# Cross-attention and a mixture of experts on one core: exponentials half a batch behind the maxima, and a first and a due step for every other stage

## The chip, the cores and the metric

One core of a Trainium2 chip (trn2). The engines named below are PE (TensorE, matrix products and transposes), DVE (VectorE), ACT (ScalarE), POOL (GpSimd) and SP (SyncE, which here only issues DMAs). The metric is the time of one execution on the device in microseconds (us), as the median over runs. All data is 32-bit float.

## The reference, cut to what matters

`x` is 8 batches of 256 tokens of width 512, `ctx` the same. Norms have no learned scale.

```python
x = x + xattn(layernorm(x), ctx, ctx)   # q: 32 heads of 16; k, v: 8 groups, each shared by 4 heads
                                        # softmax(q k^T / 4) v, then @ Wfc.T + bfc
h = layernorm(x)
scores = softmax(h @ gate_weight.T)     # 8 experts in 4 pairs: the two best pairs, the two best experts
routed = sum over the two experts of  w * (silu(h @ g.T) * (h @ u.T)) @ d.T     # inner width 352
shared = (silu(h @ sg.T) * (h @ su.T)) @ sd.T                                   # inner width 704
x = x + routed + shared
```

## The kernel before, in words

Order of execution on PE, ACT, DVE and SP is the order in which the program issues instructions (`manual_schedule`); each engine works its own queue in that order. All work of the first stage is done batch by batch (256 tokens, two row tiles of 128), and the kernel interleaves several batches by hand.

**The stages of one batch.**
- `project(b)`: normalizes x (moments, a power on POOL, two rows), products for keys and values (`pkv`), transposes (`tx`, `tk`), products for queries (`pq`, 512 wide), transposes (`tq`) into `qT`. Keys and queries carry a 17th row: in `kT` it is all ones, in `qT` it is filled later with minus the row maximum, so that the exponential needs no separate subtraction.
- `maxima(b)`: eight units per batch. A unit makes 1024 scores per query row group (L598, into the one PSUM buffer `ps_s` of four banks), and DVE reduces them to negated row maxima `nm` (L606). After every second unit `place` transposes these (`tn`) and DVE adds them into `qT` (L588).
- `softmax(b)`: eight units. A unit makes transposed scores (L667, into the same `ps_s`), ACT takes the exponential (L675, 128x2048), PE multiplies with the values (`av`, L626, `values`); every second unit DVE copies the sum (`avs`), PE transposes it (`to`), and DVE divides by the row sum (`divide`). Here `av` of unit k is issued after the scores of unit k+1.
- `close(b)`: loads x again as `acc`, POOL adds the bias, transposes of the attention output (`too`), the output product (`fc`, L701), DVE adds it to `acc`, then `layernorm`, transposes (`th`) into `hT`.
- `router(b)`: gate product (`lg`, 16 products of 8 columns), some twenty small DVE operations for the choice of experts, a product for the places (`pos`), more small DVE operations, then four indirect DMAs from POOL that scatter the rows to the experts' lists in DRAM (`rows`).
- `feed.pieces(b)`: the shared feed-forward: six pairs of products (`gu`, 3.45 us of PE each), ACT's tanh, two DVE operations, then two output products (`o`, L166), a DVE add and the write of `y`.

PSUM for everything but scores and `av` comes from `ps_m`, three buffers in turn.

**What sets the order.** The main loop runs b = 0 to 7, each with eight steps. A step issues one unit of `maxima(b + 1)` and one of `softmax(b)`, so exponentials follow the maxima by a whole batch; before b = 0 stands a loop of `maxima(0)` with `project(1)` alone. The other stages are generators that yield pieces of 0.44 to 1.72 us of PE time. A `Filler` holds those of this b (`feed.pieces(b - 2)`, `router(b - 2)`, `project(b + 2)`, `close(b - 1)`), spreads their whole cost evenly over the eight steps (0.6 of a step's share after the maxima's scores, 0.4 at the step's end), takes the stage that is least advanced, and drains what is left after the eighth step. `copy.free` says whether PSUM copies go to ACT (first part of a step) or DVE (second part). A piece that yields True leaves a product open, and the same stage goes on.

**The end.** After b = 7 come `close(7)`, `router(6)`, `router(7)` and `feed.pieces(6)`, `plan()` (some 35 DVE operations that make the tables of the routed stage, and eight more scatters), and `routed`: 39 tiles of 128 rows, each an expert's rows fetched with a DMA (`xs`, whose row number is read from a table), transposed (`rx`), multiplied (`rg`, `ro`) and added into `y` by an indirect DMA. `feed.pieces(7)` is threaded through its first lines (L331 and on).

Of the kernel before, what the change touches and what calls it, by code (L numbers as in the profile page):

```python
# [37 lines left out]
P = 128  # L38
# [22 lines left out]
PAUSE = 0.01, False  # L61

# [118 lines left out]
class Filler:  # L181
# [3 lines left out]

    def __init__(self, *stages):
        self.stages = [[g, total, 0.0, ahead] for g, total, ahead in stages]
        self.credit = 0.0
        self.last, self.open = None, False

    def total(self):
        return sum(s[1] for s in self.stages)

    def step(self):
        s = self.last
        if not self.open:
            others = [t for t in self.stages if t is not self.last]
            s = min(others or self.stages, key=lambda t: t[2] / (t[1] * t[3]))
        piece = next(s[0], None)
        if piece is None:  # L200
            self.stages.remove(s)
            return
        cost, self.open = piece
        s[2] += cost
        self.credit -= cost
        self.last = s

    def fill(self, amount):
        self.credit += amount
        while self.stages and self.credit > 0:  # L210
            self.step()

    def drain(self):
        self.fill(1e9)
# [13 lines left out]
def routed(ctx, tc, ps_m, wgu, wd, ident, rows, t_exp, t_row, t_one, out, tail, right):  # L228
# [104 lines left out]
    advance(tail, 3)  # L333
# [6 lines left out]
    advance(tail, 12)  # L340
    turn(0)
    for _ in tail:
        pass
# [18 lines left out]


def advance(stage, n):
    for _ in range(n):
        next(stage)


def attention(
# [109 lines left out]
    def layernorm(tiles, b, key, width, bufs):  # L479

        mv = small.tile([P, QC, 2], F32, tag=f"mv{key}", name=f"mv{key}{b}")
        for q in range(QC):
            st = small.tile([P, 6], F32, tag="st", name=f"st{key}{b}_{q}")
            nc.vector.bn_stats(st, tiles[q])
            nc.vector.bn_aggr(mv[:, q], st)
        rstd = small.tile([P, QC], F32, tag=f"rstd{key}", name=f"rstd{key}{b}")
        nc.vector.tensor_scalar(rstd, mv[:, :, 1], EPS, None, ALU.add)
        nc.gpsimd.tensor_tensor(rstd, rstd, mhalf, ALU.pow)
        normed = []
        for q in range(QC):  # L490
            n = small.tile([P, width], F32, tag=f"row{key}", bufs=bufs, name=f"ln{key}{b}_{q}")
            nc.vector.tensor_scalar(
                n[:, :D], tiles[q], mv[:, q, 0:1], rstd[:, q : q + 1], ALU.subtract, ALU.mult
            )
            normed.append(n)
        return normed
# [11 lines left out]
    def project(b):  # L508

        xt, cT = loaded.pop(b)  # L510
        normed = layernorm(xt, b, "a", D, 2)
# [52 lines left out]
        qT = p3.tile([P, NG, GH, S], F32, tag="qT", name=f"qT{b}")  # L564
# [11 lines left out]
    def maxima(b):  # L576


        qT, kT = qTs[b], kTs[b]

        def place(G, j0):
            ps = ps_m.tile([P, 2, S], F32, tag="m", name=f"tn{b}_{G}_{j0}")
            for j in range(2):
                for qc in range(QC):
                    nc.tensor.transpose(
                        ps[:, j, qc * P : (qc + 1) * P], nm[qc][:, G, j0 + j], ident
                    )
            nc.vector.tensor_add(qT[:, G, j0 : j0 + 2], ps, qT[:, G, j0 : j0 + 2])  # L588

        ready = []  # L590
        for G in range(NG):
            for j0 in range(0, GH, 2):
                for qc in range(QC):
                    ps = ps_s.tile([P, 4, 2, S], F32, tag="s", name=f"s1_{b}_{G}_{qc}_{j0}")
                    for j in range(2):
                        for r in range(4):
                            band = slice(32 * r, 32 * r + KA)
                            nc.tensor.matmul(  # L598
                                ps[:, r, j],
                                lhsT=qT[band, G, j0 + j, qc * P : (qc + 1) * P],  # L600
                                rhs=kT[band, G],
                                start=True,
                                stop=True,
                            )
                    to = nm[qc][:, G, j0 : j0 + 2].rearrange("p j (r x) -> p r j x", x=32)
                    nc.vector.tensor_reduce(to[:, :, :, 0], ps, AX.X, ALU.max, negate=True)  # L606
                    yield
                    if ready:
                        place(*ready.pop())
                    yield  # L610
                ready.append((G, j0))
        place(*ready.pop())

    def softmax(b):

        qT, kT, v = qTs.pop(b), kTs.pop(b), vs[b % 3]
        o = [p2.tile([P, D], F32, tag=f"o{qc}", name=f"o{b}_{qc}") for qc in range(QC)]
        os_[b] = o
        avs_ = {}

        def values(G, j0, kc, ex):
            if kc == 0:
                avs_[G, j0] = ps_av.tile([P, 2, S], F32, tag="av", name=f"av{b}_{G}_{j0}")
            av = avs_[G, j0]
            for r in range(4):
                nc.tensor.matmul(  # L626
                    av[32 * r : 32 * r + 32],
                    lhsT=v[:, kc, 4 * G + r],
                    rhs=ex[:, r],
                    start=(kc == 0),  # L630
                    stop=(kc == QC - 1),
                )
            if kc == QC - 1:
                sb = p2.tile([P, 2, S], F32, tag="avs", name=f"avs{b}_{G}_{j0}")
                nc.vector.tensor_copy(sb, av)
                return G, j0, sb

        def divide(G, j0, sb):
            ps = ps_m.tile([P, QC, 2, 4, 32], F32, tag="m", name=f"to{b}_{G}_{j0}")
            for qc in range(QC):  # L640
                for j in range(2):
                    nc.tensor.transpose(
                        ps[:, qc, j].rearrange("p r d -> p (r d)"),
                        sb[:, j, qc * P : (qc + 1) * P],
                        ident,
                    )
            rec = small.tile([P, QC, 2, 4, 1], F32, tag="rec", name=f"rec{b}_{G}_{j0}")
            nc.vector.reciprocal(rec, ps[:, :, :, :, HD : HD + 1])
            half = D // NG
            for qc in range(QC):  # L650
                to = o[qc][:, G * half : (G + 1) * half].rearrange(
                    "p (r j d) -> p j r d", r=4, j=GH
                )
                nc.vector.tensor_mul(
                    to[:, j0 : j0 + 2],
                    ps[:, qc, :, :, :HD],
                    rec[:, qc].to_broadcast([P, 2, 4, HD]),
                )

        behind, done = [], []  # L660
        for G in range(NG):
            for j0 in range(0, GH, 2):
                for kc in range(QC):
                    ps = ps_s.tile([P, 4, 2, S], F32, tag="s", name=f"s2_{b}_{G}_{kc}_{j0}")
                    for r in range(4):
                        band = slice(32 * r, 32 * r + KA)
                        nc.tensor.matmul(  # L667
                            ps[:, r],
                            lhsT=kT[band, G, kc * P : (kc + 1) * P],
                            rhs=qT[band, G, j0 : j0 + 2],  # L670
                            start=True,
                            stop=True,
                        )
                    ex = p2.tile([P, 4, 2, S], F32, tag="ex", name=f"ex{b}_{G}_{kc}_{j0}")
                    nc.scalar.activation(ex, ps, AF.Exp, scale=HD**-0.5)  # L675
                    yield
                    if done:
                        divide(*done.pop())
                    if behind:
                        done.append(values(*behind.pop()))  # L680
                        if done[-1] is None:
                            done.pop()
                    behind.append((G, j0, kc, ex))
                    yield
        last = values(*behind.pop())
        yield
        divide(*last)

    def close(b):
# [4 lines left out]
        o = os_.pop(b)  # L694
        for qc in range(QC):
            oT = p2.tile([P, NC, P], F32, tag="oT", bufs=1, name=f"oT{b}_{qc}")
            transposed(o[qc], oT, f"too{b}_{qc}")
            yield 0.44, False
            ps = ps_m.tile([P, D], F32, tag="m", name=f"fc{b}_{qc}")
# [180 lines left out]
    for _ in project(0):  # L880
        pass
# [3 lines left out]
    for k, _ in enumerate(maxima(0)):  # L885
        if k % 2 == 0:
            other.fill(share)
# [100 lines left out]
```

## Time and profile before

| | us |
|---|---|
| median of 3 runs (1120.47 to 1550.64) | 1124.05 |
| the profiled execution, whole | 1115.04 |
| its span, first to last instruction | 1113.3 |
| PE busy | 1046.5 (94%) |
| DVE busy | 476.9 (43%) |
| ACT busy | 225.3 (20%) |
| POOL busy | 143.4 (13%) |
| mean granted TensorE clock | 0.97 |

The page gives busy times over the whole span and, in 40 slices of 27.8 us, each engine's busy tenths and the clock that PE was granted. Groups of instructions carry the line in the kernel, the engine, what is written from what, and the mean duration; an idle time before an instruction is put down to what released it last. `x8` after a product in the timeline counts 32-bit products twice, as two passes each. PE's records overlap by about 0.1 us, so that the distance from start to start is the price of an instruction in a row of them. Memory traffic is 67 GB/s on average and 14.2% of the DMA engines' time for the main queue.

### The profile page before, as it was taken

To read this page: it belongs to the slowest core of one execution; us is meant where nothing else is said; L and a number is where in the kernel's file an instruction comes from. 1 tells how busy PE (TensorE), PEld (TensorE's weight loads), DVE (VectorE), ACT (ScalarE), POOL (GpSimd) and SP (SyncE) were. 2 spreads that over 40 slices of the span, in tenths; PEclk is the share of its full clock that TensorE was granted. 3 is DMA by queue.
4 is the path that set the end of the run, shared out by engine and by line. 5 is a ranking of instruction groups with operands and counts; after the bars stand their busy time and mean duration, and the time that the engine had idled before them with its cause. 6 is when DMAs were issued, how large, how long until landed. Compare 5 with 4: busy or idle time off the path is not lost. (4 is left out here: it accounts for less than half of the span.)

```text
span 1113.3 us, 13379 instructions
## 1 busy us (share of the span) xinstructions
PE 1046.5 (94%) x5291; PEld 604.2 (54%) x5291; DVE 476.9 (43%) x1082; ACT 225.3 (20%) x276; POOL 143.4 (13%) x168
## 2 busy tenths in 40 slices
PE   6877899999999999999999999999999999999994
PEld 4542435554564555465455464667556566666652
DVE  3743546644654644555455534362122222222221
ACT  2132223222222122122222232110111111111110
POOL 3000000110000011101001101032012121211212
PEclk9988899998999999999899999999999999999998
DMA  5510010110200011101000101128963333233323
GB/s 199 199 38 1 15 44 1 57 40 9 67 4 36 20 58 39 39 1 40 10 29 30 49 1 49 29 82 322 376 201 69 67 60 75 58 77 58 75 32 38
DMA packets 26733, 74.94 MB, mean 67 GB/s; under 512 B 3376, under 2 KB 3376, under 8 KB 25392
## 3 DMA queue, kind: packets, MB, share of 16 engines
q1 hardware_dynamic: 17856, 53.04, 14.2%
q0 software_dynamic: 8816, 21.04, 8.5%
q8 instruction: 43, 0.70, 0.3%
q14 instruction: 18, 0.15, 0.0%
HBM read 48.31 MB, written 25.76 MB: 67 GB/s over the span
## 5 line engine op out<-in xcount | busy, mean ns | idle before, releaser
L286 PE MATMUL rg<-wgu_all,rxT 128*128 (+1 forms) x624 | 191.2, 459 | 0.3 <-issue 0.2
L606 DVE TENSOR_REDUCE nm<-s 128x8 f32<-128x2048 f32 x64 | 146.5, 2289 | 61.0 <-PE s L598 60.9
L675 ACT ACTIVATE ex<-s 128x2048 f32<-128x2048 f32 x64 | 120.2, 1877 | 195.4 <-PE s L667 195.4
L286 PEld LDWEIGHTS rg<-wgu_all,rxT 128*128 128x128 f32 x624 | 115.5, 190 | 58.4 <-issue 0.7
L314 PE MATMUL ro<-wd_all,raT 128*128 (+3 forms) x234 | 107.1, 593 | 1.7 <-DVE raT L304 1.7
L323 POOL DMA_INDIRECT y<-ry,rid x39 | 60.5, 1553 | 284.6 <-DVE ry L322 219.7
L166 PE MATMUL o<-wsd,act 128*128 128x512 f32 (+1 forms) x192 | 93.1, 626 | 0.0
L667 PE MATMUL s<-qT,kT 17*128 17x512 f32 x512 | 75.4, 659 | 18.5 <-DVE nm L606 18.2
L142 PE MATMUL gu<-hT,gate 128*128 128x256 f32 (+1 forms) x384 | 92.0, 382 | 0.3 <-ACT hT L225 0.3
L142 PE MATMUL gu<-hT,up 128*128 128x256 f32 (+1 forms) x384 | 91.6, 381 | 0.0
L296 DVE TENSOR_TENSOR ract<-rg,rsg 128x352 f32<-128x352 f32 x39 | 20.4, 524 | 156.6 <-PE rg L286 156.6
L598 PE MATMUL s<-kT,qT 17*128 17x256 f32 x1024 | 74.8, 406 | 10.9 <-DVE nm L606 5.7
L142 PEld LDWEIGHTS gu<-hT,up 128*128 128x128 f32 (+1 forms) x384 | 68.5, 181 | 19.4 <-issue 6.7
L142 PEld LDWEIGHTS gu<-hT,gate 128*128 128x128 f32 (+1 forms) x384 | 66.8, 181 | 21.0 <-issue 9.5
L626 PE MATMUL av<-ex,v 128*32 128x512 f32 x512 | 72.1, 637 | 0.0
L598 PEld LDWEIGHTS s<-kT,qT 17*128 17x128 f32 x1024 | 47.0, 187 | 46.1 <-issue 28.1
L314 PEld LDWEIGHTS ro<-wd_all,raT 128*128 128x128 f32 (+1 forms) x234 | 44.4, 190 | 47.3 <-issue 37.3
L269 ACT COPY rxT<-rx 128x512 f32<-128x512 f32 x39 | 22.8, 585 | 201.4 <-PE rx L267 201.4
L322 DVE TENSOR_SCALAR ry<-ro,rw 128x512 f32<-128x512 f32 x39 | 29.3, 750 | 78.9 <-PE ro L314 78.9
L701 PE MATMUL fc<-wfc_sb,oT 128*128 128x512 f32 x128 | 61.0, 608 | 2.0 <-DVE oT L225 1.8
L551 PE MATMUL pq<-wq_sb,xT 128*128 128x512 f32 x128 | 62.1, 617 | 0.0
L166 PEld LDWEIGHTS o<-wsd,act 128*128 128x128 f32 (+1 forms) x192 | 36.6, 202 | 42.6 <-issue 42.0
(156 smaller groups left out, 912.6 us busy)
## 6 DMA issues: line engine op xcount, KB each, us to landing
wgu_all<-wgu SPq DMA_DIRECT2D x8, 1408.0 KB, 13.1
xs<-rows SPq DMA_DIRECT2D x39, 264.0 KB, 3.0
wd_all<-wd SPq DMA_DIRECT2D x8, 768.0 KB, 7.4
x<-x SPq DMA_DIRECT2D x16, 256.0 KB, 2.8
cT<-ctxT SPq DMA_DIRECT2D x8, 512.0 KB, 5.5
acc<-x SPq DMA_DIRECT2D x16, 256.0 KB, 2.7
y<-acc SPq DMA_DIRECT2D x16, 256.0 KB, 2.0
wsd<-wsd SPq DMA_DIRECT2D x2, 768.0 KB, 11.3
```

The costliest lines, as they stand in the source:

```text
L142: nc.tensor.matmul(ps[:fn, i], lhsT=self.gu[e][i][:, c, f0 : f0 + fn], rhs=hT[:, c], start=(c == 0), stop=(c == NC - 1),)
L166: nc.tensor.matmul(ps, lhsT=act[:fn, e, fc, q * P : (q + 1) * P], rhs=self.down[e][:fn, fc], start=(e == 0 and fc == 0), stop=(e == N_SH - ...
L286: nc.tensor.matmul(gu[k], lhsT=xT[:, c], rhs=w.rearrange("p o f -> p (o f)"), start=(c == 0), stop=(c == NC - 1),)
L314: nc.tensor.matmul(o, lhsT=aT[:fn, fc], rhs=w.rearrange("p o d -> p (o d)"), start=(fc == 0), stop=(fc == len(FCH) - 1),)
L323: nc.gpsimd.indirect_dma_start(out=out, out_offset=bass.IndirectOffsetOnAxis(ap=ids.pop(i), axis=0), in_=y, in_offset=None, compute_op=ALU ...
L551: nc.tensor.matmul(ps.rearrange("p h d -> p (h d)"), lhsT=xT[:, c, qc * P : (qc + 1) * P], rhs=wq_sb[:, c], start=(c == 0), stop=(c == NC ...
L598: nc.tensor.matmul(ps[:, r, j], lhsT=qT[band, G, j0 + j, qc * P : (qc + 1) * P], rhs=kT[band, G], start=True, stop=True,)
L606: nc.vector.tensor_reduce(to[:, :, :, 0], ps, AX.X, ALU.max, negate=True)
L626: nc.tensor.matmul(av[32 * r : 32 * r + 32], lhsT=v[:, kc, 4 * G + r], rhs=ex[:, r], start=(kc == 0), stop=(kc == QC - 1),)
L667: nc.tensor.matmul(ps[:, r], lhsT=kT[band, G, kc * P : (kc + 1) * P], rhs=qT[band, G, j0 : j0 + 2], start=True, stop=True,)
L675: nc.scalar.activation(ex, ps, AF.Exp, scale=HD**-0.5)
L701: nc.tensor.matmul(ps, lhsT=oT[:, c], rhs=wfc_sb[:, c], start=(c == 0), stop=(c == NC - 1))
```

## The change

It does four things.

1. One loop runs over steps k = -4 to 63. Step k issues unit k + 4 of the maxima (`LAG = 4`, half a batch) and unit k of the exponentials. `values(k, ex)` is issued at the end of the same step, after the fill; `divide(k - 1)` at every even step, `place` at every odd one.
2. `Filler` is replaced by `Others`. Each stage has a first step and a due step, and is stepped only while its share of cost done is below the share of time gone plus 0.02. Credit of a step that finds no stage below its line is dropped. What is due is finished before the step. `project(b)` runs from 8b - 12 to 8b - 4; with end = 8(b + 1), `close(b)` from end + 0.4 to end + 3.6, `router(b)` from end + 4 to end + 8, `feed.pieces(b)` from end + 5 to end + 13. A step may fill at most 7.6 us.
3. `layernorm` is split: in `close` each row tile's moments are issued right after its `fc` add, and the rest (`normalised`) two pauses ahead of the transposes; both `too` transposes come ahead of both `fc` products, with two `oT` buffers.
4. `avs` is copied by ACT, `qT` has two buffers in place of three, batches of x and ctx are loaded at steps 7, 15 and so on, and the end is issued by `Stage` pieces: `feed.pieces(7)` begins inside `router(7)` once `feed.pieces(6)` is over.

```diff
-class Filler:
...
+class Stage:
+    def __init__(self, pieces, total, start, due):
...
+    def ahead(self, now):
+        return self.cost / self.total - (now - self.start) / (self.due - self.start)
+class Others:
...
+    def fill(self, now, amount):
+        self.credit = min(self.credit, 0.0) + amount
+        while self.credit > 0:
+            some = [s for s in self.stages if s.start <= now and s.ahead(now) < LEAD]
+            if not some:
+                break
+            some = [s for s in some if s is not self.last] or some
+            self.step(min(some, key=lambda s: s.ahead(now)))
...
+    def finish_due(self, now):
+        for s in [s for s in self.stages if s.due <= now]:
+            self.finish(s)
...
-    def layernorm(tiles, b, key, width, bufs):
+    def moments(mv, tile_, q, key):
+    def normalised(tiles, mv, b, key, width, bufs):
...
-        qT = p3.tile([P, NG, GH, S], F32, tag="qT", name=f"qT{b}")
+        qT = p3.tile([P, NG, GH, S], F32, tag="qT", bufs=2, name=f"qT{b}")
...
-                nc.vector.tensor_copy(sb, av)
+            nc.scalar.copy(sb, av)
...
             nc.vector.tensor_add(acc[qc], ps, acc[qc])
+            moments(mv, acc[qc], qc, f"f{b}")
             yield 1.72, False
-        n_rows = layernorm(acc, b, "f", W, 4)
+        n_rows = normalised(acc, mv, b, "f", W, 4)
+        for _ in range(2):
+            yield PAUSE
...
+    for b in range(1, B):
+        others.add(project(b), PROJECT, UNITS * b - 3 * LAG, UNITS * b - LAG)
+    for b in range(B - 1):
+        end = UNITS * (b + 1)
+        others.add(close(b), CLOSE, end + 0.4, end + 3.6)
+        rt = others.add(router(b), ROUTER, end + 4, end + 8)
+        sh = others.add(feed.pieces(b), feed.TOTAL, end + 5, end + 13)
+    amount = 7.6
+    n = B * UNITS
+    for k in range(-LAG, n):
+        if k % UNITS == UNITS - 1 and (k + 17) // UNITS < B:
+            b = (k + 17) // UNITS
+            loaded[b] = load_batch(b)
+        if k == 0:
+            feed.load()
+        others.finish_due(k)
+        copy.free = "ACT"
+        if k + LAG < n:
+            maxima(k + LAG)
+            others.fill(k, 0.6 * amount if k >= 0 else amount)
+        copy.free = "DVE"
+        if k >= 0:
+            ex = weights(k)
+        if k + LAG < n and k % QC == QC - 1:
+            place(k + LAG)
+        if k > 0 and k % QC == 0:
+            divide(k - 1)
+        if k >= 0:
+            others.fill(k + 0.4, 0.4 * amount if k + LAG < n else amount)
+            values(k, ex)
```

In the text below, "position" is k modulo 8: the place of a step within a batch.

## The prediction

> **What bounds the kernel now.** I read the page's overview first, then busy time by stage, then PE's waits, then the timeline where a wait sits.
>
> ```profile
> PE   6877899999999999999999999999999999999994
> DVE  3743546644654644555455534362122222222221
> PEclk9988899998999999999899999999999999999998
> ```
>
> PE is the bound from slice 5 on. Before that it is neither full nor at full clock. By stage (columns: stretch, its length, then PE, PEld, DVE, ACT, POOL busy, then the granted clock):
>
> ```profile
> 57.16:129.24 72.08, 56.57 (x346) 26.29 (x345) 31.43 (x36) 18.56 (x16) 0.69 (x1) 0.81 0.05 15
> 129.24:188.94 59.70, 54.77 (x384) 25.84 (x380) 35.51 (x49) 20.47 (x18) 4.21 (x8) 1.00 0.09 27
> 282.97:376.25 93.28, 89.31 (x524) 50.20 (x520) 48.45 (x100) 22.28 (x23) 8.50 (x12) 0.98 0.10 35
> ```
>
> These are the loops b=0, b=1 and b=3. To see what a stage must cost I add PE's program order at its issue distances in the timeline: a 512-wide product 0.86 us, 256-wide 0.43, a transpose 0.11, `lg` 1.77, the 8 maxima products ("s1", L598) 1.08, the 4 exponential products ("s2", L667) 1.07, the 4 `av` products 1.00. The whole program is 985.5 us, in both kernels: no product is added or removed. 8.2 us pass before the first product and 20.8 after the last, so before loses 1113.3 - 985.5 - 29.0 = 98.8 us. By stage: before L598 starts at 24.1, 2.5; the maxima-only loop 33.1 for 23.8 of work (9.3 lost); b=0 30.5; b=1 9.0; b=2 to 5 some 93.5 each for 83.8 (38.6 together); b=6 4.3; the rest 4.6.
>
> What PE waited for (total, times, longest):
>
> ```profile
> PE s L667 <- DVE nm L606: 18.2, 14, 2.4
> PE th L502 <- DVE lnf L492: 9.3, 5, 2.1
> PE s L598 <- ACT ex L675: 5.0, 5, 2.0
> ```
>
> The price of the first and last, where nothing stands between:
>
> ```profile
> 92.03 1.15 PE L598 MATMUL s<-kT,qT 17*128 17x256 f32 x16
> 95.59 1.14 PE L667 MATMUL s<-qT,kT 17*128 17x512 f32 x8 [2.42 <-DVE nm L606]
> 140.32 1.14 PE L667 MATMUL s<-qT,kT 17*128 17x512 f32 x8
> 143.52 1.15 PE L598 MATMUL s<-kT,qT 17*128 17x256 f32 x16 [1.06 <-ACT ex L675]
> ```
>
> Both share one `ps_s` buffer. From s1's end to s2: 95.59 - 92.03 - 1.08 = 2.48 us (the reduction, 2.29, and two hand-overs). From s2's end until its exponential is done: 143.52 - 140.32 - 1.07 = 2.13. PE must hold 2.48 us of other work after s1 and 2.13 after s2.
>
> **The change part by part.** (1) *`av` moves.* Before, `av` of the previous unit fills the time under an exponential. Now `values(k, ex)` follows its own exponential in PE's order, with only place or divide (0.44) and a 0.4 fill between; behind the waiting `av` stand the rest of the fill and the next s1. A step with no fill in the second half costs 1.08 + 2.48 + 1.07 + 2.13 + 1.00 = 7.76 us.
>
> (2) *Rationed filling.* A stage is stepped only while under its due line. In k=0 to 7 only projection is open: 13.4 us over 8 steps, so every step is light. Seven at 7.76 and one at 8.2: 62.5 us for 41.6 of work. The same formula (without `av` after the wait) gives b=0 of before 59.4, and it took 72.08 at clock 0.81; I add the same 12.7: 75.2. Steps -4 to -1 are the reduction's, as now: 27.75 - 24.10, then one held 5.75 by projection's normalization, then about 4: 17.6 for 11.7. Halving the lag saves half of the maxima-only loop (15 us), but k=8 to 15 become what b=1 was: 75.1 by the formula, 2.0 for `th` and 1.7 for the router on DVE (below), 3 of clock: 82 for 64.9. Lost to k=15: 2.5 + 5.9 + 33.6 + 17.1 = 59; before lost 51 up to b=1's end.
>
> (3) *The dense batches, k=16 to 47.* One batch is 83.8 us of PE work, as now. By position in the batch the built order gives: at 5, 1.72 of `gu` after s1; at 6, 0.87 before `av`, 1.26 short; at 7, 0.44 before `av`, 1.69 short. Position 5 is worse than the formula, as DVE is late. Position 4 issues the router's `lg`, and with project's first step its normalization, before the next maxima; DVE works in order. The same queue in before:
>
> ```profile
> 288.00 1.85 PE L737 MATMUL lg<-wg_sb,hT 128*128 128x8 f32 x16
> 294.50 0.17 DVE L767 TENSOR_TENSOR score<-score,sel 128x16 f32<-128x16 f32 x1
> 298.21 0.42 DVE L225 COPY ktok<-pkv 128x256 f32<-128x256 f32 x1
> 298.88 2.28 DVE L606 TENSOR_REDUCE nm<-s 128x8 f32<-128x2048 f32 x1
> 301.22 1.14 PE L667 MATMUL s<-qT,kT 17*128 17x512 f32 x8 [1.53 <-DVE nm L606]
> ```
>
> From `lg`'s end (289.78) the router takes 4.9, the normalization 3.6, two copies 0.7, the reduction 2.3: s2 comes 11.44 later. Before holds s2, pkv 3.45, s1, too and gu between and waits 1.5. Now pkv 1.72, av 1.00, pkv 1.72, s1 1.08 and gu 1.72 stand there: 7.24, a wait of 4.2. At position 3 `th` still waits on `lnf`: the moments moved ahead to `fc`, but rstd, POOL's power (0.7) and two rows (1.1) queue on DVE behind the reduction, an add, `qT`'s add and one `tq` copy. Adding those from s2: `lnf` at +5.0, PE there at +2.8: 2.2, and 0.8 more for the second `th`, whose PSUM buffer waits on a `tq` copy behind `lnf`. At position 0 `too` directly follows the divide it reads (reciprocal and two products): 1.1. Sum: 4.2 + 1.26 + 1.69 + 3.0 + 1.1 = 11.2 idle, against 2.9 now (length less PE busy, mean of the four). The other 6.8 that before loses there, clock and issue, I keep: 101.8 per batch, 407 for four.
>
> (4) *The end.* k=48 to 55: 75.6 of work, 10.0 idle by the same positions (no projection: 3.5 at position 5), 3.4 clock: 89. k=56 to 62: 59.7 + 3.8 + 2 = 65.5. The rest is 383.4 of work plus 3 for small waits. The routed stage's first rows need a chain:
>
> ```profile
> 743.38 0.38 PE L776 MATMUL pos<-sel,ones 128*128 128x16 f32 x2
> 745.92 0.96 POOL L804 DMA_INDIRECT rows<-lnf,idx  x1 [8.30 <-DVE idx L798]
> 759.82 0.96 POOL L804 DMA_INDIRECT rows<-empty,b_idx  x1 [0.30 <-issue]
> 768.67 1.47 SPq L261 DMA_DIRECT2D xs<-rows  x2
> ```
>
> Twelve POOL scatters take 15.2; SP's load then waits for them to land, and lands after 3.5 at best: 28.5 after `pos`. Now 32.7 us of PE work (o 6.88, six gu pairs 20.7, o 5.16) cover it. In the changed order one gu pair and the o rows came before: 17.2 + 5.16 = 22.4, so `rx` waits up to 6.1. With `y` of the seventh batch and the `wgu` loads off SP earlier, the scatters might land in 3 instead of 8: 1.5. Taken: 4, nearer the row.
>
> Edits that cost nothing: `avs` on ACT (0.59 for DVE's 0.69; ACT is busy 22 of 93 us); two `oT` (no wait on the first); `qT` with two buffers, since batch b+2 is written four steps after batch b's last s2; loads at step 7, five steps ahead of use (5.5 us to land). close takes its two `acc` loads on SP and two bias sums on POOL (1.27 each) along to position 0; on SP they stand behind `y` of two batches before, written by position 4 of the last batch, and the sum is read some 15 us later. The router's four scatters (5.1 us of POOL) sit at position 6, five steps before the next POOL power at 3, which waits for none. Without that cover each would hold project for those 5.5.
>
> **Sum, on the profiled span.** 24.1 + 17.6 + 75.2 + 82 + 407 + 89 + 65.5 + 390.4 + 20.8 = 1171.6, 58 more than 1113.3. With 1.7 around the span: 1173.3. The runs' median is 1124.05 where this execution took 1115.04; the same ratio gives 1183.
>
> **The clock, by row and by rule.** Two stretches of 3.4 us, columns as above; the granted clock is third from the right. In the first PE waited 2.0 us on an exponential:
>
> ```profile
> 61.20:64.60 3.40, 1.40 (x16) 0.67 (x12) 2.17 (x7) 1.88 (x1) 0.69 (x1) 0.84 0.00 0
> 64.60:68.00 3.40, 3.40 (x21) 2.31 (x14) 1.98 (x1) 0.00 (x0) 0.00 (x0) 0.50 0.78 264
> ```
>
> The Trainium skill, "TensorE: Matmul & The Clock Gate", section "What's actually happening", has the array fall to half clock after an idle window of some 3.4 us. No wait here is longer than 2.4 after the first product, yet it fell. By the rule only position 5's 4.2 would drop the clock and k=0 to 7 would run at full speed: 12.7 less, 5 x 1.7 more, about 1179. By the row every 2 us wait may: my sum. It speaks against the change, which adds such waits in either reading.
>
> **Rivals.** *More clock lost:* each new wait costs one more window at half clock (1.7). Two per batch over six batches: 1183 + 20 = 1203, and twice that at worst. For: the front at 0.81. Against: b=1 of before waits 4.9 us in all and keeps 1.00. *DVE catches up:* the waits at 3, 5 and 0 shrink to the formula's, since a PE held up once gives DVE time: up to 3.4 + 3.0 + 1.1 = 7.5 per batch, 37 over five, 1146 at the least; I take 1153. Against: the row at 301.22 shows that queue already not caught up. *Not slower:* the clock. Before loses about 6.8 per dense batch and 12.7 in b=0 beyond its waits; if the evener mix of small and large products kept it at 1.00, then 4 x 6.8 + 12.7 + 3 + 3.4 + 2 = 48 goes: 1135, within 2%. It decides once 37 of the 48 are gone. For: b=1 runs at 1.00 with a mixed order and 8% idle. Against: b=0, whose light steps k=0 to 7 repeat. That the lag isn't halved can't be: the built order has the first s2 after five s1, where it had nine.
>
> **How the numbers follow.** As summed 0.56 (own range 1155 to 1205), more clock lost 0.16, DVE catches up 0.13, not slower 0.12, faster by something unseen 0.03. A measurement of this kernel tells about 2% from no change (1101.6 to 1146.5). Faster 0.04, same 0.15 (a part of the DVE case with it), slower 0.81. Range 1138 to 1216.
>
> **What would show it.** Right: in each dense batch one s2 wait on `nm` near 4 us after `lg`; `av` waiting on `ex` twice a batch; `th` still waiting; light steps of 7.8 us or more up to k=7. Wrong: s2's wait on `nm` staying under 2, or a clock of 1.00 from 41 to 116 us.

## The result, and the profile after

The changed kernel takes 1185.56 us (median; 1182.67 to 1187.56) where the kernel before takes 1122.26 on the same chip: 1.058 times as long, 95% interval 1.0525 to 1.064. (The median of before counts one slow run of 1550.64, which the ratio leaves out.) Its profiled execution took 1182.67 us, its span is 1181.0 (before 1113.3), the mean granted clock 0.943 (before 0.970).

First the overview, the same three rows as were read of before:

```profile
PE   6778899998999898899889799999899999999995
DVE  3543464455355445444544544335222222222221
PEclk9798879998999998899899789799999999999998
```

PE is no longer at 9 from slice 5 to the end of the batches, and the clock row has new 7s and 8s in the same slices. The page gives PE 1077.4 us of busy time, before 1046.5. So of 67.7 us more span, 30.9 are the same products running slower and 36.8 are idle time. The stages (stretch, length, then PE, PEld, DVE, ACT, POOL busy, then granted clock): k=0 to 7, k=8 to 15, the four dense batches k=16 to 47, k=48 to 55, k=56 to 62.

```profile
47.13:115.32 68.19, 53.13 (x345) 24.66 (x344) 29.44 (x33) 20.42 (x18) 3.19 (x3) 0.87 0.10 33
115.32:203.50 88.18, 79.61 (x457) 41.91 (x453) 43.34 (x87) 23.40 (x25) 8.34 (x12) 0.86 0.09 31
203.50:304.62 101.12, 92.66 (x521) 51.73 (x521) 49.29 (x99) 22.24 (x23) 8.20 (x12) 0.95 0.09 32
304.62:401.10 96.48, 89.68 (x521) 50.48 (x521) 49.25 (x99) 22.25 (x23) 8.51 (x12) 0.98 0.10 34
401.10:503.96 102.86, 94.43 (x522) 52.18 (x521) 49.25 (x99) 22.24 (x23) 8.51 (x12) 0.93 0.09 32
503.96:605.88 101.92, 91.77 (x521) 51.26 (x521) 50.97 (x99) 22.25 (x23) 8.60 (x12) 0.95 0.06 22
605.88:702.21 96.33, 87.52 (x485) 47.63 (x485) 46.84 (x89) 20.49 (x20) 7.87 (x11) 0.89 0.07 23
702.21:774.22 72.01, 68.78 (x360) 37.33 (x357) 29.63 (x64) 18.20 (x18) 3.93 (x7) 0.91 0.04 15
```

A dense batch has some 520 PE instructions, 83.8 us of work, as before. It now takes 100.6 us on average in place of 93.5. PE's waits (what waits, for what: total, times, longest):

```profile
PE s L643 <- DVE nm L622: 26.8, 14, 5.3
PE av L662 <- ACT ex L651: 26.1, 20, 2.0
PE th L524 <- DVE lnf L514: 11.3, 7, 2.3
```

The first row was 18.2 with no wait over 2.4, the second did not exist, the third was 9.3. In the timeline the long wait stands where the prediction put it, at position 5 behind `lg`:

```profile
261.28 1.85 PE L755 MATMUL lg<-wg_sb,hT 128*128 128x8 f32 x16
267.78 0.17 DVE L785 TENSOR_TENSOR score<-score,sel 128x16 f32<-128x16 f32 x1
271.50 0.42 DVE L251 COPY ktok<-pkv 128x256 f32<-128x256 f32 x1
272.17 2.28 DVE L622 TENSOR_REDUCE nm<-s 128x8 f32<-128x2048 f32 x1
274.50 2.09 PE L643 MATMUL s<-qT,kT 17*128 17x512 f32 x8 [3.62 <-DVE nm L622]
```

From `lg`'s end (263.05) to s2: 11.45 us; the prediction's sum was 11.44. Note the last row's duration: 2.09 for products that take 1.14 elsewhere. The same place in stretches of 3.41 us, columns as above:

```profile
267.24:270.65 3.41, 3.41 (x27) 2.37 (x26) 2.41 (x9) 0.00 (x0) 0.69 (x1) 1.00 0.00 0
270.65:274.06 3.41, 0.23 (x2) 0.00 (x0) 3.41 (x5) 0.00 (x0) 0.00 (x0) 1.00 0.54 171
274.06:277.47 3.41, 2.97 (x13) 1.46 (x14) 0.39 (x1) 0.75 (x1) 0.27 (x1) 0.50 0.81 291
277.47:280.88 3.41, 3.41 (x9) 2.32 (x8) 0.69 (x1) 1.12 (x1) 2.22 (x2) 0.50 0.00 0
280.88:284.30 3.42, 3.42 (x31) 2.03 (x31) 1.98 (x3) 0.97 (x2) 0.00 (x0) 1.00 0.02 5
```

PE is busy for 0.23 us in one stretch, and in the next two it has half the clock: the work that they do in 6.8 us would take 3.2 at full clock (2.97 and 3.41 busy, halved). A wait of 3.6 us here costs 3.6 and nearly as much again.

### The profile page after: what moved, and what is told of

It is laid out like the page before. It is cut to its first block, busy times and chain, and to the rows that moved or that the text cites. A ratio compares the mean times of both kernels' runs of the same rounds, so it can differ in the third digit from the quotient of the medians.

```text
span 1181.0 us, 13377 instructions
## 1 busy us (share of the span) xinstructions
PE 1077.4 (91%) x5291; PEld 616.3 (52%) x5291; DVE 479.2 (41%) x1072; ACT 231.5 (20%) x286; POOL 143.7 (12%) x168
## 4 chain that ended last, share of the span: by engine, by line
PE 51%; issue 32%; DVE 8%; POOL 4%; DMA 2%; ACT 2%; POOLq 0%; SPq 0%; DVEq 0%; ACTq 0%
PE rg L312 15%; PE ro L340 8%; PE gu L145 6%; PE o L169 3%; DVE nm L622 3%; PE s L614 3%; PE av L662 3%; PE s L643 3%; POOL rows L822 3%; ACT ex L651 2%; PE pq L576 2%; PE rx L293 1%; PE fc L712 1%; PE ra L328 1%; DMA xs<-rows 1%
## 5 line engine op out<-in xcount | busy, mean ns | idle before, releaser
L643 PE MATMUL s<-qT,kT 17*128 17x512 f32 x512 | 77.8, 678 | 26.8 <-DVE nm L622 26.8
L662 PE MATMUL av<-ex,v 128*32 128x512 f32 x512 | 78.0, 685 | 26.2 <-ACT ex L651 26.1
L145 PE MATMUL gu<-hT,gate 128*128 128x256 f32 (+1 forms) x384 | 96.8, 396 | 0.0
L145 PE MATMUL gu<-hT,up 128*128 128x256 f32 (+1 forms) x384 | 96.1, 395 | 0.0
L614 PE MATMUL s<-kT,qT 17*128 17x256 f32 x1024 | 82.0, 438 | 2.0 <-DVE nm L622 2.0
L145 PEld LDWEIGHTS gu<-hT,gate 128*128 128x128 f32 (+1 forms) x384 | 68.1, 186 | 24.5 <-issue 11.6
L145 PEld LDWEIGHTS gu<-hT,up 128*128 128x128 f32 (+1 forms) x384 | 71.7, 190 | 16.8 <-issue 3.3
L614 PEld LDWEIGHTS s<-kT,qT 17*128 17x128 f32 x1024 | 51.0, 204 | 52.4 <-issue 48.1
## 6 DMA issues: line engine op xcount, KB each, us to landing
wsd<-wsd SPq DMA_DIRECT2D x2, 768.0 KB, 12.7
```

Source lines behind the costliest of these rows:

```text
L145: nc.tensor.matmul(ps[:fn, i], lhsT=self.gu[e][i][:, c, f0 : f0 + fn], rhs=hT[:, c], start=(c == 0), stop=(c == NC - 1),)
L614: nc.tensor.matmul(ps[:, r, j], lhsT=qT[band, G, j0 + j, qc * P : (qc + 1) * P], rhs=kT[band, G], start=True, stop=True,)
L643: nc.tensor.matmul(ps[:, r], lhsT=kT[band, G, kc * P : (kc + 1) * P], rhs=qT[band, G, j0 : j0 + 2], start=True, stop=True,)
L662: nc.tensor.matmul(av[32 * r : 32 * r + 32], lhsT=vs[b % 3][:, kc, 4 * G + r], rhs=ex[:, r], start=(kc == 0), stop=(kc == QC - 1),)
```

## The experiments

The theory: the loss is (a) light front steps in which `av` waits for its own exponential, (b) DVE's queue at position 5 (router and normalization ahead of one reduction), `th` right behind its normalization, and the exponentials at positions 6 and 7, (c) half clock behind these waits. The rivals: (a) alone; the clock for its own reasons; the half lag itself. Each run is compared with runs of the kernel before on its own chip (medians 1117.6 to 1122.4), so the ratio carries between groups of runs; beside it stands the median.

**`av` one step later.**

```diff
+            if k > 0:
+                values(k - 1, behind)
             others.fill(k + 0.4, 0.4 * amount if k + LAG < n else amount)
-            values(k, ex)
+            if k > 0 and k % QC == 0:
+                divide(k - 1)
+            behind = ex
```

> The changed kernel with the values product one step later: av of unit k-1 follows the scores of unit k, as in the kernel before, divide moves to the end of its step, close starts at end+1, avs is copied by DVE. Theory (the new order of av and exponential costs what PE waits on ex, 26.1 us in all): the 8 waits of k=0 to 7 and two per dense batch go, about half of it coming back as waits of the next s1 on the same ps_s buffer where little else stands under the exponential; a light step costs 6.8 instead of 7.8 us: k=0 to 7 about 60 instead of 68.2, a dense batch 2 us shorter, the whole 1155 to 1165. Rival (DVE's queue and the clock make the loss, av only waits where PE would wait anyway): above 1178.

Measured 1175.48, ratio 1.052 (1.0463 to 1.0577): between the two expectations. The front did what the theory says: k=0 to 7 in 61.55 us instead of 68.19, k=8 to 15 in 79.25 instead of 88.18. The dense batches lost by it (102.4 to 105.1, where the changed kernel has 96.5 to 102.9): the `av` waits went and new ones came, in the whole run 12.7 us in 12 waits of `to` on `avs`, as divide now follows its copy at once, and up to 7.1 at position 5. The order of `av` costs in the front; in the dense batches this run tells nothing clean, since it made waits of its own.

**The router one step later.**

```diff
-        rt = others.add(router(b), ROUTER, end + 4, end + 8)
+        rt = others.add(router(b), ROUTER, end + 5, end + 8)
```

> The changed kernel with the router's first step at end+5 instead of end+4, so that lg and its 4.9 us of DVE no longer stand with project's normalization ahead of one reduction. Theory (DVE's queue at position 5): the wait of s2 on nm at position 5, 3.6 us on average, falls under 0.5; position 6 rises from 1.0 to about 2.2, as the router now stands ahead of that reduction; net 2.4 us a batch over six batches and a little clock: 1165 to 1172. Rival (the queue is only handed on, DVE's work per step is the limit): 1180 to 1188. Rival (each wait near 4 us costs a window of half clock as well): under 1160.

Measured 1129.85, ratio 1.0115 (1.0057 to 1.0172). One number takes back 51 of the 63 us (12 are left over its own runs of before). Of the three expectations only the last rival's range, under 1160 for half clock on top of each long wait, contains it. A dense batch of this kernel, and PE's waits in all four of them:

```profile
196.36:288.79 92.43, 89.23 (x525) 50.09 (x521) 50.76 (x100) 22.26 (x23) 8.52 (x12) 0.98 0.10 35
```

```profile
PE th L524 <- DVE lnf L514: 6.1, 4, 1.6
PE s L643 <- DVE nm L622: 3.7, 5, 1.0
PE too L524 <- DVE o L691: 1.8, 4, 0.5
PE th L524 <- DVE qT L251: 1.3, 4, 0.3
```

In the changed kernel the same view of k=16 to 47 has 14.6 for s2 on `nm` (longest 5.3) and 10.0 for `av` on `ex`; here 3.7 (longest 1.0) and none. Position 6, for which 2.2 was expected, waits 0.99 at most. By stage against the changed kernel: k=8 to 15 6.8 less, the dense batches 33.5, k=48 to 55 10.1, k=56 to 62 1.5, k=0 to 7 nothing. That `av`'s waits went too is the pacing's doing: with the router later, `gu` products and `pos` fall into the second part of positions 6 and 7. So this run mixes two causes, and the next takes them apart.

**Only DVE's order at that place.** `lg` stays; the twenty DVE operations come at the stage's next pull.

```diff
         shape = [P, QC, N_EXP]
+        yield 0.4, False
         top = small.tile([P, QC, 1], F32, tag="top", name=f"top{b}")
...
-        yield 0.9, False
+        yield 0.5, False
```

> The changed kernel with the router's twenty DVE operations one pull of the stage later: lg stays where it is, PE's order is the same instruction for instruction, and DVE has the chain behind position 5's reduction instead of ahead of it. Theory (DVE's order at that one place): the wait of s2 on nm at position 5 (3.6 on average) goes to 0, and with it the half clock of the products behind it, some 3 us; over six batches 1138 to 1150, with av's waits at positions 6 and 7 (1.0 and 1.5) still there. Rival (router_late won by its other mix of products, which filled positions 6 and 7): 1165 or more.

Measured 1163.64, ratio 1.0383 (1.0326 to 1.044): a third of the loss. That lies outside the theory's range and 1.4 us short of the rival's. By stage the theory holds where it speaks: in the dense batches PE's instructions and their order are those of the changed kernel, and the three batches k=16 to 39 take 93.84, 93.66 and 93.62 us, 6.5 less than the changed kernel's mean of 100.2 over these three, at clock 1.00 (the fourth 96.61, 5.3 less). Position 5 waits 0.49, and `av`'s 10.0 us of waits are still there. So DVE's order alone gives some 6.2 of the 8.4 us per batch that router_late gains. But k=0 to 7 took 77.72 and k=8 to 15 93.63, though PE's instructions are the same up to step 12 (in step 13 one group of `gu` products comes ahead of s2). The rows of k=0 to 7, k=8 to 15 and one dense batch:

```profile
43.62:121.34 77.72, 63.31 (x345) 28.06 (x345) 29.33 (x33) 20.43 (x18) 3.19 (x3) 0.73 0.09 32
121.34:214.97 93.63, 83.03 (x456) 44.76 (x452) 43.30 (x87) 23.33 (x25) 8.36 (x12) 0.84 0.08 29
308.81:402.47 93.66, 88.12 (x521) 49.53 (x520) 50.88 (x99) 22.27 (x23) 8.52 (x12) 1.00 0.10 35
```

**The front's clock.** Two runs move router_split's work by products nobody reads, ahead of step -4: three, then one.

```diff
+    ps = ps_m.tile([P, D], F32, tag="m", name="shift")
+    for i in range(3):
+        nc.tensor.matmul(ps, lhsT=ident, rhs=wq_sb[:, i], start=True, stop=True)
     for k in range(-LAG, n):
```

> router_split with three products nobody reads (2.6 us of PE) ahead of step -4. router_split gained 7.5 us in each dense batch as expected, but its k=0 to 7 took 77.7 us where the changed kernel, with the same instructions there, took 68.2, and k=8 to 15 93.6 instead of 88.2; only the granted clock differs (0.73 and 0.87), and its first maxima began at 23.5 instead of 25.9. Theory (the clock is granted in stretches of 3.4 us on a fixed grid, and it is the place of the waits against that grid that decides which of them cost a half-clock stretch): moved by 2.6 us, k=0 to 7 falls to 68 to 72 and the whole to 1145 to 1155. Rival (the moved router chain itself slows the front or the runs before it): 1163 to 1168.

Measured 1166.11, ratio 1.043 (1.0365 to 1.0495); k=0 to 7 took 78.2. The theory missed, and the rival's range (1163 to 1168) holds the number. (The dense batches of router_split had gained 6.2 on average, not the 7.5 named there.) The first maxima began at 27.56 and not 26.1: the first products came 0.2 us later and ran 1.1 longer.

> router_split with one product nobody reads (0.86 us) ahead of step -4. split_shift did not settle its question: with three products the first maxima began 4.03 us later, and 4.03 is one stretch of the clock's grid (3.41) and 0.6, so that the work lay against the grid nearly as before. One product should move it by a quarter of a stretch. Theory (the place against the grid decides which waits of the front cost half clock): k=0 to 7 leaves 77.7, and 68 to 73 is likely; the whole 1145 to 1158. Rival (something in the moved chain keeps the front slow wherever it lies): k=0 to 7 stays at 77 to 79 and the whole at 1162 to 1168.

Measured 1158.73, ratio 1.0364 (1.0314 to 1.0415), just over the range; k=0 to 7 took 68.17. The first maxima began 3.1 us later, not 0.9, as the first products waited 1.7 longer for their load. So the moved chain is not to blame: with it the same steps take 68 or 78 us. The dense batches lost some of it again (96.7, 95.2, 96.6, 98.2).

These shifts can't be read from the start of the span, as the expectation just shown does for split_shift, because the clock's edges lie elsewhere in each execution. Every change of the clock falls on one grid of 3.41 us, which begins at 1.04 us of the span in router_split, 0.13 in split_shift, 0.22 in split_shift1 and 0.98 in the changed kernel. Counted from the last edge before it, step 0 begins at 1.62, 1.05, 1.89 and 1.78, and the eight steps take 77.7, 78.2, 68.2 and 68.2. Against the grid the first maxima of split_shift lie 1.5 us later than in router_split, and not "nearly as before". The traces of router_split and the changed kernel part at one wait of `av`, 1.41 us in both. Stretches of 3.41 us close to the clock's own edges, first router_split, then the changed kernel:

```profile
55.60:59.02 3.42, 2.08 (x13) 0.73 (x12) 0.69 (x1) 1.86 (x1) 0.00 (x0) 0.99 0.00 0
59.02:62.43 3.41, 3.34 (x24) 1.42 (x24) 0.00 (x0) 0.60 (x2) 0.00 (x0) 0.51 0.00 0
62.43:65.84 3.41, 3.41 (x12) 1.18 (x4) 2.29 (x1) 0.00 (x0) 0.00 (x0) 0.50 0.00 0
```

```profile
59.02:62.43 3.41, 2.17 (x14) 0.73 (x12) 0.69 (x1) 1.76 (x1) 0.00 (x0) 1.00 0.00 0
62.43:65.84 3.41, 3.24 (x27) 1.56 (x28) 1.03 (x1) 0.70 (x2) 0.00 (x0) 1.00 0.00 0
```

1.34 us idle within one stretch (3.42 less 2.08) was followed by half clock; the same wait, cut by an edge so that 1.24 fell into one stretch, was not. It would be easy to call the edge the cause, but router_late has the same wait whole inside one stretch, 1.41 us idle, and keeps full clock behind it:

```profile
58.91:62.32 3.41, 2.00 (x20) 0.69 (x17) 0.69 (x1) 1.88 (x1) 0.00 (x0) 1.00 0.00 0
62.32:65.74 3.42, 2.95 (x20) 1.29 (x20) 2.29 (x1) 0.96 (x2) 0.00 (x0) 1.00 0.00 0
```

Its step 0 begins at 1.57, next to router_split's 1.62, and its eight steps take 68.1. This is the zone in which both happen (last section). The runs show that the same steps differ by 10 us where only the granted clock differs; that their place on the grid decides this they do not show.

**Products under the waits.** The changed kernel with 44.7 us of products nobody reads (at full clock) where PE waits.

```diff
+        if 8 <= k < 56 and k % UNITS == 5:
+            dummy(k, 4)
         if k >= 0:
             ex = weights(k)
...
+            if 0 <= k < 8:
+                dummy(k, 2)
+            elif k < 56 and k % UNITS in (6, 7):
+                dummy(k, 1)
             values(k, ex)
```

> The changed kernel plus products nobody reads (128x512 into a ps_m buffer) where PE waits: two ahead of av in k=0 to 7, four ahead of s2 at position 5 and one ahead of av at positions 6 and 7 in k=8 to 55: 16 + 24 + 12 = 52 products, 44.7 us of PE at full clock. It tells the price of the waits from that of the clock. Theory (the waits set the time, a lower clock comes on top where PE has idled): the products hide in the waits for the most part, PE's clock rises in k=0 to 7 from 0.87 towards 1.00 and the whole lies at 1160 to 1185. Rival (PE's work sets the time, the waits in the trace are slack of the product before): 1215 to 1230. Rival (the clock falls for the mix of work and not for the idle time): 1183 to 1200 with the clock unchanged.

Measured 1156.8, ratio 1.0358 (1.03 to 1.0416), below the theory's range: with 44.7 us more work the kernel is 2.2 points of ratio faster, some 25 us. The mean clock is 0.98. In k=40 to 47 and k=48 to 55 the stages fall from 101.92 to 98.20 and from 96.33 to 91.13. The waits were real idle time, and filling them raised the clock, against the rival that expected it unchanged. (The added products also change the mix of work; what speaks for the idle time itself is the count in the last section.) In k=0 to 7 the time goes from 68.19 to 66.82 with 13.8 us of products added and the clock from 0.87 to 0.97: all of them fit under DVE's and ACT's time.

**The half lag undone alone.**

```diff
-LAG = 4
+LAG = 8
...
-        others.add(project(b), PROJECT, UNITS * b - 3 * LAG, UNITS * b - LAG)
+        others.add(project(b), PROJECT, UNITS * b - 2 * LAG, UNITS * b - LAG)
```

> The changed kernel with LAG = 8, three qT buffers, loads four steps earlier and project from 8b-16 to 8b-8: the half lag alone is undone; stages, av, moments and avs stay as changed. Theory (the half lag saves the maxima-only steps, about 15 us, and costs little by itself; with it undone project's normalization moves from position 4 to 0 and the wait at position 5 shrinks by 2 to 3.6 a batch): 1175 to 1190. Rival (the half lag itself is what costs): under 1140.

Measured 1157.85, ratio 1.0367 (1.0289 to 1.0445): faster than the theory's range, far from the rival. The maxima-only loop is 17.6 us longer (38.86 for 21.24) and k=0 to 7 8.6 longer, but k=16 to 47 takes 374.5 instead of 402.4. `project` now begins at position 0, and its normalization no longer stands with the router. Of the 7.0 us per batch, s2 at position 5 gives 2.0 (it still waits 1.7), `th`, which waits no more, 1.8, `av` and `too` 0.7, and PE's shorter busy time the other 2.5. The clash is thus one part of it; that `th`'s wait would go had not been allowed for.

**`avs` back on DVE.** `nc.scalar.copy(sb, av)` becomes `nc.vector.tensor_copy(sb, av)`.

> The changed kernel with avs copied by DVE, as before. Theory (costed at nothing in the prediction): within 5 us of the changed kernel's 1185, the place of the waits against the clock's grid may move it that far. Rival (ACT's copy delays exponentials or av): under 1175.

Measured 1175.24, ratio 1.0488 (1.0447 to 1.0529). That is 10 us, or 0.9%, under the changed kernel, more than the 5 allowed and just short of the rival; the two intervals touch. In its profile k=16 to 47 takes 403.5 us (402.4 in the changed kernel); the single stages go both ways by 4, at clocks that differ. Nothing in the traces ties it to ACT's queue; I leave open whether the copy costs something or only moves the work against the clock; one profiled execution of each can't tell, since the same steps differ by 10 us in router_split and split_shift1.

**Toward a better order.** Three kernels on router_late: `th` later, the front's `av` one step later, and both.

```diff
-        others.add(close(b), CLOSE, end + 0.4, end + 3.6)
+        others.add(close(b), CLOSE, end + 0.4, end + 4.2)
```

> router_late with close due at end+4.2 instead of end+3.6: th is issued at the end of position 4 behind av and not at position 3 right behind the normalization. Theory (a wait costs its length and the half clock behind it): th's waits, 1.5 and 0.3 a batch, and the slower av, tq and s1 behind them, 1.6, go in six batches: 20 us under router_late, 1108 to 1114 where router_late has 1130. Rival (th's wait is slack of DVE's queue and comes back at the next reduction): 1124 to 1132.

Measured 1112.58, ratio 0.9939 (0.9916 to 0.9963), as the theory says. What it removes, in the changed kernel's timeline (router_late has the same):

```profile
248.62 0.63 PE L524 MATMUL th<-ident,lnf 128*128 128x128 f32 x4 [1.55 <-DVE lnf L514]
249.58 0.65 PE L524 MATMUL th<-ident,lnf 128*128 128x128 f32 x4 [0.33 <-DVE qT L251]
250.16 1.93 PE L662 MATMUL av<-ex,v 128*32 128x512 f32 x8
```

After 1.9 us of waits, `av` takes 1.93 instead of 1.06.

```diff
+            if 0 < k <= FRONT:
+                values(k - 1, behind)
             others.fill(k + 0.4, 0.4 * amount if k + LAG < n else amount)
-            values(k, ex)
+            if k >= FRONT:
+                values(k, ex)
+            behind = ex
```

> router_late with av one step later in k=0 to 7 only (divide of such a unit at the next odd step). Theory: a light step falls from 7.7 to 6.8 us as av lies under the next exponential; k=0 to 7 in 61 instead of 68.1 us, everything else as in router_late: 1121 to 1125 where router_late has 1130. Rival (av's wait there is made good elsewhere): 1128 to 1132.

Measured 1121.6, ratio 1.0001 (0.9982 to 1.002); k=0 to 7 takes 61.45 instead of 68.14, as expected.

> router_late, rl_th and rl_front together. If the three gains stand in different stages they add: 1100 to 1106, under the kernel before by 1 to 1.5%. If th's gain comes back elsewhere: 1118 to 1124.

Measured 1099.51, ratio 0.9818 (0.9774 to 0.9862), half a us below the range: the gains add, and the kernel is 1.8% faster than the one before. Its second dense batch (the four take 88.7, 88.9, 88.9 and 94.6; in the last `lg` waits 1.7 on `hT`, and half clock follows):

```profile
271.28:360.21 88.93, 87.45 (x524) 49.62 (x520) 50.97 (x100) 22.24 (x23) 8.52 (x12) 1.00 0.10 37
```

**The half lag in that order.** rl_th_front with LAG = 8 and the edits of lag8.

> rl_th_front with LAG = 8, three qT buffers, loads four steps earlier and project from 8b-16 to 8b-8, as lag8: what the half lag is worth once the clash of router and normalization, th's wait and the front's av are mended. Theory (the half lag saves maxima-only steps and nothing else): 1099.5 plus the 17.6 us by which lag8's maxima-only loop was longer: 1112 to 1122. Rival (half the lag costs by itself, as it puts project's first step at position 4): under 1102.

Measured 1111.21, ratio 0.9921 (0.9892 to 0.9951), below the range by 0.8. With the clash gone the half lag is worth 1.0%, some 12 us: 18.5 in the maxima-only loop (38.9 for 20.4), less what the batches behind it give back.

## Why the prediction was right, and where its sizes were off

1183 was forecast, 1185.56 measured, and the mechanisms are those named. That the number is so close is luck, twice over. On the profiled span the sum was 1171.6 against 1181.0, 9.4 short; the ratio by which before's median lay above its profiled execution then added 9.5, where this kernel's median lies only 2.9 above its own. And within the sum terms that were off by up to 14 us partly cancel:

| step of the prediction | predicted | measured |
|---|---|---|
| first maxima | 24.1 | 25.9 |
| k=-4 to -1 | 17.6 | 21.2 |
| k=0 to 7 | 75.2 | 68.2 |
| k=8 to 15 | 82 | 88.2 |
| k=16 to 47 | 407 | 402.4 |
| k=48 to 62 | 154.5 | 168.3 |
| rest and end | 411.2 | 406.8 |

- *The light step, "7.76 us"*: right. At full clock k=4 takes 7.75 (80.64 to 88.39 in the timeline of the changed kernel). The order of `av` is some 0.8 us of it: rl_front gains 6.7 over the eight steps.
- *"the same 12.7" of clock in k=0 to 7*: mis-sized. The amount was carried over from a stage with clock 0.81. The profile shows 5.7 over 62.5 at clock 0.87, router_split 15.2 with the same instructions at 0.73. Only part of the slower products shows in the length: PE's busy time is 11.5 over its work, but the idle time is 15.1 of 20.9 forecast, as the rest of the slow products lies where PE would have waited for DVE or ACT.
- *k=-4 to -1*: `tn` waits 2.6 on the reduction at 35.30 and half clock follows; of this I had seen only the waits.
- *"3 of clock" in k=8 to 15 and "3.4 clock" in k=48 to 55, 2 in k=56 to 62*: these are the terms that failed most. PE's busy time over its work (some issue time among it) is 14.7 in k=8 to 15 and 21.0 in k=48 to 62. The idle times were forecast too high (13.9 for 8.6; 13.8 for 12.0), which hid a part. (The "10.0" among them adds up to 10.5 by its own terms.) A wait's price is its length and the half clock behind it; I priced the second only as what before had shown.
- *The dense batch, "11.2 idle" and "6.8 kept"*: position 5 3.6 on average (1.99 to 5.34, predicted 4.2), position 6 1.03 (1.26), position 7 1.47 (1.69), `th` 1.8 (3.0), `too` 0.46 (1.1): 8.4 of 8.5 idle. Clock and issue 8.3 instead of 6.8. The queue of router and normalization is confirmed twice: by 11.45 us from `lg`'s end, and by router_split, which leaves PE's order in these batches alone and gains 6.2 a batch (3.9 in split_shift1, the same batches at a lower clock).
- *`rx`, "taken: 4"*: 4.5, but not in the form told. The first tile waits 0.56; the third waits 3.99, as its load is issued only at 847.39, behind a write of `y` that SP waited for.
- *The edits costed at nothing*: `avs` on ACT stays open by 10 us (above); none of the others shows a wait of its own.
- *The clock by row or by rule*: the row was right. Full clock was lost after waits of 1.4 to 2.6 us, far under an idle window of 3.4. (The longest wait of before after its first product was 2.7, of s1 on `nm` at 33.50, and not 2.4; that changes nothing here.)
- *Rivals*: "more clock lost" is what happened in k=48 to 62, "DVE catches up" shows once, at position 5 of the second dense batch (1.99). "Not slower" by a clock at 1.00 did not happen, and it took too much for the clock's: at a clock of 1.00 a dense batch of rl_th_front keeps PE busy for 87.4 us for 83.8 of work, so of the 6.8 that before loses beyond its waits only about 3 are the clock's. It also lacked a reason for the clock to rise: the waits must go first.

What I did not see is how much hung on one number. With the waits mended the half lag gains about 1% by itself (lag8_best against rl_th_front). The changed kernel's loss of 5.8% goes with one first step (router_late: 4.7 points of ratio), then `th` (1.8 points) and the front's `av` (1.2 points). Of the 4.7 points, router_split shows 2.0 for the two stages that stood ahead of one reduction, with k=0 to 15 slowed by 15 us at a lower clock; how the rest divides between the other pacing and the clock was not taken apart.

## What to carry to other kernels

When stages get fixed first steps, write down per position what the in-order vector engine must do before the next reduction that the matrix engine waits for; two stages that begin at one position are one queue, and one step's offset was worth some 50 us here. Price a wait of the matrix engine at its length plus, in most cases, a half-clock stretch behind it if it leaves more than 1.5 us of a 3.4 us stretch idle. Where another engine sets the step, some of the slow products hide under its time (in k=0 to 7 about half), so the clock's loss and the waits must not simply be added. And compare a stage of two kernels at the clock that each was granted: the same steps took 68 or 78 us here.

## What the runs showed of the hardware

In each trace the clock changes only on a grid of 3.41 us that begins at another time of the span in each execution (0.98 us in the changed kernel, 2.05 in the kernel before), which agrees with the free-running window of the Trainium skill's "TensorE: Matmul & The Clock Gate", section "What's actually happening". But a whole idle window is not needed. I cut the changed kernel's trace into such stretches at the clock's own edges: of 17 full-clock stretches with more than 1.5 us idle, 16 were followed by half clock; of 264 with less than 0.9, 2; of the 17 between, 3. In the fourteen traces together, counted likewise, it is about 116 of 142, 24 of some 3840 and 55 of 205: over 1.5 us half clock is likely but not certain (router_late 8 of 11, router_split 7 of 11), between 0.9 and 1.5 either may come, and what decides is not shown.

Half-clock stretches number 17 of 316 in the kernel before, 37 of 336 in the changed one, 20 of 321 in router_late and 11 of 312 in rl_th_front. 20 more at 1.7 us each are 34 us, near the 30.9 that PE's busy time grew. And the same eight steps took 77.7 us at clock 0.73, 78.2 at 0.71 and 68.2 at 0.87 (router_split, split_shift, split_shift1): 10 us, 0.9% of the kernel, that no edit of these steps made.
